# Denominators of a graph attention: some weight tiles summed on GpSimd, fewer by ones on TensorE, and the transfers' sum closed in the next block

## The chip, the cores and the metric

One core of a Trainium2 chip runs the whole program. The metric is the device time of one execution in microseconds, the median of three; the profile is one profiled execution of the same program. The engines are named as in the profile: PE is TensorE, DVE is VectorE, ACT is ScalarE, POOL is GpSimd, SP is the engine whose queue issues most of the loads.

## The reference

Two graph layers work on 4096 nodes with 512 features each and one adjacency matrix of 4096 x 4096 zeros and ones. Each has four heads of 128 features. The change concerns the second layer, a graph attention:

```python
feats = jnp.einsum('nf,hfo->hno', X, W)
e_s = jnp.einsum('hno,ho->hn', feats, a_self)
e_n = jnp.einsum('hno,ho->hn', feats, a_neigh)
logits = e_s[:, :, None] + e_n[:, None, :]
logits = jnp.where(logits > 0, logits, LRELU_ALPHA * logits)
logits = logits + NEG_INF * (1.0 - A)[None, :, :]
attn = jax.nn.softmax(logits, axis=-1)
out = jnp.einsum('hnm,hmo->hno', attn, feats)
```

X is the normalised output of the first layer. For every target node n the softmax needs, besides the weighted sum over its neighbours m, the sum of the weights themselves: the denominator.

## The kernel before

The program runs a first stage (normalisation, projections), an encoder attention, a feed-forward block, a decoder attention, a second block, and at the end the attention of the second layer ("gat"). All three attentions share one function, `attention` (L210).

Its work is cut into blocks: one head h and one half tb of the targets (TB = 2048 targets), eight blocks for each attention. Inside a block a loop goes over j, 32 tiles of 128 neighbours. For each j a weight tile e of 128 neighbours x 2048 targets in fp32 (1 MB) is made: ACT computes it from a row of target scores (L798), and DVE adds a column and multiplies with the mask (L799, `gat_weights`); the mask `a` is one byte an element and is loaded by SP's queue. Then TensorE multiplies the values' 128 x 128 tile with the four 512-wide parts of e and accumulates over j in four PSUM banks `po` (`products`, L351; fp32, so a product appears as two matmul instructions). In the first tiles of a block only three of the four banks are free, and the fourth catches up at j = EVICT = 2 (L348).

The denominators are the column sums of all 32 weight tiles, and there are three ways for a tile to get into them. `modes(n)` says which for block n; before the change all eight blocks of the last attention use `GAT` (L64):

- *moved* (11 tiles): GpSimd issues a transfer that adds the tile, element by element, onto a tile `sums2` (L363). In the first block it is added onto a DRAM tile `dacc`, which is loaded back into a weight tile at j = 30 (L319 to L321), because `sums2` shares the memory of the first block's row. Each transfer waits for the one before it, since both change the same tile.
- *by ones* (3 tiles: 9, 30, 31): TensorE multiplies with a 128 x 32 matrix of ones and accumulates into a PSUM bank `den` (`add_to_den`, L303): four 512-wide parts side by side in four groups of 32 columns, eight instructions a tile.
- all others (18 tiles): DVE adds them to `acc` (L369 the first two, L371 the rest), which is half of the big tile R[2].

At j = 31, `sums2` and `acc` go through the ones as well, so that `den` then holds the denominators (L378 to L382).

What is to be done after a block is put into `later`, a table by tile number of the next block: at j = EVICT ACT copies the four banks out (`out_gat`, L804); at j = INVERT = 4 ACT copies `den`, and GpSimd's queue writes it to DRAM and reads it back as a column (`denominators`, L244 to L251); at j = 10 DVE takes the reciprocals and GpSimd's queue writes them (L253 to L256); from j = 11 GpSimd's queue loads them spread over all partitions (rb, L261), and six tiles later DVE multiplies the block's results with them (L808), ACT applies the bias and the ReLU (L811), and GpSimd's queue adds them to the output (L817). In the last block there is no next one, and the end is done at once (L394 to L411).

The order of instructions on each engine is that of the program's text with some pins (`tc.issue_after`). The sum by ones goes behind the products of its tile, and the next products behind it. Weight tiles go round in a ring: EP + ebufs = 2 + 7 = 9 tiles in the last attention (`weight_tile`, L237). A tile is free again when its products, and its transfer or its add, are done.

Of the kernel before, what the change touches and what calls it, by code (L numbers as in the profile page):

```python
# [31 lines left out]
FP = mybir.dt.float32  # L32
U8 = mybir.dt.uint8
AF = mybir.ActivationFunctionType
ALU = mybir.AluOpType
# [4 lines left out]
N, F, H, D, P = 4096, 512, 4, 128, 128  # L40
IB = 512
NIB = N // IB
NJ = N // P
C = IB // P

TB = 2048
NTB = N // TB
SB = TB // IB
# [8 lines left out]
TINY = 1e-30  # L57
# [1 line left out]
G_MAX = 75.0  # L59


ENC_FIRST = (), (5, 6, 10, 11, 15, 16, 20, 21, 25, 26, 30, 31)
ENC = (0, 2, 5, 7, 10, 12, 15, 17, 20, 22, 25), (8, 9, 30, 31)
GAT = (0, 2, 5, 7, 10, 12, 15, 17, 20, 22, 25), (9, 30, 31)  # L64

KEEP = 5

# [2 lines left out]
EVICT = 2  # L70
INVERT = 4
# [9 lines left out]
def kernel(ctx, tc, x, xT, adjT, w0, w0T, v0, wencT, wdecT, vecs, w1, w1T, a1, outT):  # L81
    nc = tc.nc
    consts = ctx.enter_context(tc.tile_pool(name="consts", bufs=1))
    dram = ctx.enter_context(tc.tile_pool(name="dram", bufs=1, space=DRAM))
# [5 lines left out]
    R = [big.tile([P, N], FP, name=f"R{i}") for i in range(5)]  # L90
# [12 lines left out]
    def bank1():  # L103
        return psum1.tile([P, IB], FP, name="den")
# [3 lines left out]
    ones = consts.tile([P, P], FP, name="ones")  # L108
# [38 lines left out]
    ekeep = [[[dram.tile([P, TB], FP, name=f"ekeep{h}_{t}_{k}") for k in range(NJ // KEEP)] for t in range(NTB)]  # L147
             for h in range(H)]

    dacc = dram.tile([P, TB], FP, name="dacc")  # L150

    masks = [[dram.tile([MG * P, TB], U8, name=f"mask{t}_{g}") for g in range(NJ // MG)] for t in range(NTB)]

    def everywhere(d, row, lo, n):
# [55 lines left out]
    def attention(what, keep, pools, weights, values, row_of, out, finish, ebufs, modes=None, invert=None,  # L210
# [21 lines left out]
        spool, made, masks0 = pools, 0, list(masks0)  # L232
        if invert is not None:
            acc = spool.tile([P, TB], FP, name="acc") if sums is None else sums
            sums2 = spool.tile([P, TB], FP, name="acc2") if sums2 is None else sums2

        def weight_tile():  # L237
            nonlocal made
            made += 1
            if made % (EP + ebufs) < EP:  # L240
                return keep.tile([P, TB], FP, name="e", tag="ek", bufs=EP)
            return spool.tile([P, TB], FP, name="e", bufs=ebufs)
# [15 lines left out]
        def spread(h, tb, s):  # L258
# [2 lines left out]
            nc.gpsimd.dma_start(rb, everywhere(rinvs[h][tb], 0, s * IB, IB))  # L261
            return rb

        def at(j, f, *args):

            later.setdefault(j, []).append(lambda: f(*args))

        def ending(h, tb, po, den):

            outs = [out(spool, h, tb, s, po[s]) for s in range(SB)]  # L270
            if den is not None:
                def invert_later():
                    dcol = denominators(h, tb, den)
                    at(INVERT + 6, invert_them, h, tb, dcol)

                at(INVERT, invert_later)
            rbs = {}
            for s, o in enumerate(outs):

                j = INVERT + 7 + s % 2 + s // 2 * 7  # L280
                at(j, lambda s=s: rbs.update({s: spread(h, tb, s)}))
                for k, f in enumerate(finish):
                    at(j + 6 + k, lambda f=f, s=s, o=o: f(spool, h, tb, s, o, rbs[s], False))
# [8 lines left out]
        blocks = [(h, tb) for h in range(H) for tb in range(NTB)]  # L292
        for n, (h, tb) in enumerate(blocks):
            last = n == len(blocks) - 1
            moved, by_ones = modes(n) if modes is not None else ((), ())
            if invert is not None:
                den = bank1()
                begun = False

            def add_to_den(t, stop=False):  # L300
                nonlocal begun, last_ones
                for s in range(SB):
                    last_ones = nc.tensor.matmul(den[s * 32:(s + 1) * 32, :], ones[:, 0:32], t[:, s * IB:(s + 1) * IB],  # L303
                                                 start=not begun, stop=stop)
                begun = True

            po, ahead = [bank() for _ in range(SB - 1)], []
            adds, held, back, stores, next_row = [], [], None, [], None
            for j in range(NJ):

                with pinned(products_of):
                    for f in later.pop(j, []):
                        f()
                with tc.issue_after(a_load.ins) if j else nullcontext():
                    if (n, j) in extras:
                        extras[n, j](a_load)
                    if not last and j == NJ - 10:
                        next_row = next_row_of(*blocks[n + 1])
                if n == 0 and moved and j == NJ - 2:  # L319
                    back = weight_tile()  # L320
                    nc.gpsimd.dma_start(back, dacc)  # L321
                e = weight_tile()
                store = j % KEEP == KEEP - 1 and kept is not None
                if store and kept == "read":
                    a_load = nc.sync.dma_start(e, ekeep[h][tb][j // KEEP])
                else:
                    if masks0:
                        a, a_load = masks0.pop(0)
                    else:
                        a = mask_tile(keep)  # L330
                        a_load = load_mask(a, tb, j)
                    products_of = weights(e, rowb, a, j, h, SB if n + j == 0 else 1)
                    if store:
                        stores.append((j // KEEP, e))

                    if j % KEEP == KEEP - 3 and stores:
                        k, t = stores.pop()
                        nc.scalar.dma_start(ekeep[h][tb][k], t)

                def products():  # L340
                    nonlocal last_main, last_ones

                    with tc.issue_after(last_ones.ins) if last_ones is not None else nullcontext():

                        if j == EVICT:
                            po.append(bank())
                            for k, t in ahead:
                                nc.tensor.matmul(po[-1], block(values[h], k), t[:, (SB - 1) * IB:SB * IB],  # L348
                                                 start=(k == 0), stop=False)
                        for s, b in enumerate(po):  # L350
                            last_main = nc.tensor.matmul(b, block(values[h], j), e[:, s * IB:(s + 1) * IB],  # L351
                                                         start=(j == 0), stop=(j == NJ - 1))
                    last_ones = None


                early = last and j == NJ - 1 and invert is not None
                if not early:
                    products()
                if j < EVICT:
                    ahead.append((j, e))  # L360
                if invert is not None:
                    if j in moved:
                        nc.gpsimd.dma_start(sums2 if n else dacc, e, **({"accum_op": ALU.add} if j > moved[0] else {}))  # L363
                    elif j in by_ones:
                        held.append(e)
                    else:
                        adds.append(e)
                        if len(adds) == 2:
                            nc.vector.tensor_add(acc, *adds)  # L369
                        elif len(adds) > 2:  # L370
                            nc.vector.tensor_add(acc, acc, e)  # L371

                    if held and j + 1 not in by_ones:
                        with tc.issue_after(last_main.ins):
                            for t in held:
                                add_to_den(t)
                        held = []
                    if j == NJ - 1:  # L378
                        with tc.issue_after(last_ones.ins) if last_ones is not None else nullcontext():
                            if moved:  # L380
                                add_to_den(sums2 if n else back)
                            add_to_den(acc, True)  # L382
                if early:
                    products()
            for k, t in stores:
# [2 lines left out]
                else:  # L388
                    at(EVICT, nc.scalar.dma_start, ekeep[h][tb][k], t)
            if not last:  # L390
                at(EVICT, lambda *block_end: ending(*block_end), h, tb, po, den if invert is not None else None)
                rowb = next_row
                continue
            outs = [out(spool, h, tb, s, po[s]) for s in range(SB)]  # L394
# [31 lines left out]
    with tc.tile_pool(name="keep", bufs=1) as keep:  # L426

        with tc.tile_pool(name="f_small", bufs=1) as small, tc.tile_pool(name="f_work", bufs=2) as work:
# [5 lines left out]
            for ib in range(NIB):  # L434
# [7 lines left out]
                for c in range(0, C, 1 if ib == 0 else C):  # L442
                    n = 1 if ib == 0 else C
# [375 lines left out]
    with tc.tile_pool(name="gat", bufs=1) as spool:  # L819
        x1_last = []  # L820

        def load_last(load):
            x1_last.append(spool.tile([P, TB], FP, name="rowb", bufs=2))
            nc.sync.dma_start(x1_last[0], outT[(H - 1) * P:H * P, (NTB - 1) * TB:NTB * TB])

        attention("gat", spool, spool, gat_weights, v1, lambda h, tb: (rowsg, tb * H + h), out_gat,
                  (scaled_gat, add_to_output), 7, lambda n: GAT, (N * TINY, ALU.add), sums=R[2][:, 0:TB],
                  sums2=row0, row0=row0,
                  extras={(H * NTB - 1, NJ - 10): load_last})


# [40 lines left out]
```

## Time and profile before

| | |
|---|---|
| median of three runs | 3309.0 us (3308.68 to 3311.59) |
| profiled span | 3308.6 us, granted TensorE clock 0.989 |
| last attention | from about 2366 us to the end, 943 us |
| TensorE busy in it | 928 us |
| VectorE busy in it | 908 us |
| ScalarE busy in it | 571 us |
| GpSimd busy in it | 126 us, all of it issuing transfers |
| transfer that adds a weight tile | 1 MB, 8.2 us from issue to landing |

The profile has several views. The page gives busy time by engine, the span in 40 equal slices and the chain of work that ended last. Groups of instructions are listed by line and shape as "busy us, mean ns of one | idle us of the engine just before them, and what ended that idle time". The timeline lists instructions by start and duration, equal neighbours merged ("x8"). A busy TensorE is not TensorE at its peak, since ends of matmuls are modelled; its pace is best read from the starts of successive blocks. An instruction that stands still after it has begun, because something it needs is taken, counts as busy and shows only as a longer duration.

### The profile page before, as it was taken

Reading aid. Unit: us, or ns where it says so; the run is one execution under the profiler, and the core shown is the slowest. Engines: PE = TensorE matmul, PEld = TensorE weight load, DVE = VectorE, ACT = ScalarE, POOL = GpSimd, SP = SyncE. Lnnn points to the kernel's source line nnn. Section 1 sums busy time; section 2 is a strip of 40 time slices with the busy share of each in tenths; the row PEclk is TensorE's granted clock in tenths of the full one; section 3 lists DMA queues with packets and bytes.
Section 4 is the critical chain, followed back from the end, with each engine's and each line's share of the span. In section 5 each row is a group of like instructions: output and inputs, shape, how many; then the busy total and the mean of one; then the engine's idle time right before and its main releaser. Section 6 shows DMA issues by size and latency. Waiting matters only on the chain.

```text
span 3308.6 us, 25868 instructions
## 1 busy us (share of the span) xinstructions
PE 3226.6 (98%) x8847; PEld 1492.2 (45%) x8847; DVE 2677.1 (81%) x1912; ACT 2602.9 (79%) x1908; POOL 329.1 (10%) x478
## 2 busy tenths in 40 slices
PE   7989999999999999999999999999999999999999
PEld 6434434434443464444444444448644444444443
DVE  6989899999998675555655666586599989999997
ACT  7999999999997448999999999565656566566563
POOL 2000110110110000000000000024201111111111
PEclk9999999999999999999999999999999999999999
DMA  9994888988986013333443443232389779778876
GB/s 207 196 187 147 249 225 231 248 224 227 248 238 186 4 45 137 135 129 137 152 140 124 137 153 133 66 134 75 82 199 223 174 194 221 192 193 208 216 190 147
DMA packets 180164, 558.54 MB, mean 169 GB/s; under 512 B 20356, under 2 KB 23684, under 8 KB 144192
## 3 DMA queue, kind: packets, MB, share of 16 engines
q0 software_dynamic: 43088, 210.09, 32.9%
q1 hardware_dynamic: 126288, 293.66, 26.2%
q10 hardware_dynamic: 10656, 53.15, 4.0%
q8 instruction: 69, 1.13, 0.1%
q14 instruction: 63, 0.52, 0.0%
HBM read 378.15 MB, written 95.82 MB: 143 GB/s over the span
## 4 chain that ended last, share of the span: by engine, by line
PE 67%; DVE 16%; issue 9%; ACT 5%; DMA 3%; DVEq 0%; ACTq 0%; POOL 0%; POOLq 0%
PE ps L351 52%; PE ps L566 7%; DVE e L421 4%; DVE e L799 4%; DVE R L371 4%; PE ps L743 3%; ACT e L419 2%; PE den L303 2%; DVE acc L371 2%; ACT e L420 2%; DMA a<-mask 2%; PE ps L622 1%; PE ps L348 1%; PE ps L500 1%; DMA rb<-rinvs 1%
## 5 line engine op out<-in xcount | busy, mean ns | idle before, releaser
L351 PE MATMUL ps<-e,R 128*128 128x512 f32 x6048 | 2640.7, 597 | 51.8 <-DVE e L421 39.9
L351 PEld LDWEIGHTS ps<-e,R 128*128 128x128 f32 x6048 | 1147.4, 191 | 1536.4 <-issue 1417.3
L421 DVE TENSOR_TENSOR e<-e,a 128x2048 f32<-128x2048 f32 (+1 forms) x470 | 1052.3, 2260 | 403.6 <-ACT e L420 381.6
L419 ACT ACTIVATE e<-rowb,score 128x2048 f32<-128x2048 f32 (+1 forms) x470 | 912.6, 1968 | 91.3 <-PE ps L351 58.0
L420 ACT ACTIVATE e<-e 128x2048 f32<-128x2048 f32 (+1 forms) x470 | 871.0, 1880 | 17.5 <-DVE e L421 11.1
L798 ACT ACTIVATE e<-rowb,nq,jcol 128x2048 f32<-128x2048 f32 x224 | 457.9, 2086 | 225.2 <-DMA w<-e 130.1
L799 DVE SCALAR_TENSOR_TENSOR e<-e,jcol,a 128x2048 f32<-128x2048 f32 (+1 forms) x259 | 591.5, 2319 | 4.5 <-DMA a<-mask 2.7
L371 DVE TENSOR_TENSOR R<-R,e 128x2048 f32<-128x2048 f32 x128 | 292.5, 2285 | 0.0
L371 DVE TENSOR_TENSOR acc<-acc,e 128x2048 f32<-128x2048 f32 x126 | 287.9, 2285 | 1.8
L566 PE MATMUL ps<-R,w 128*128 128x512 f32 x512 | 220.3, 592 | 0.6 <-DVE w L534 0.6
L261 POOL DMA_DIRECT2D rb<-rinvs x88 | 58.7, 683 | 1095.6 <-DVE R L524 904.8
L566 PEld LDWEIGHTS ps<-R,w 128*128 128x128 f32 x512 | 97.2, 190 | 122.7 <-issue 118.2
L363 POOL DMA_DIRECT2D w<-e x77 | 64.6, 839 | 643.6 <-DMA w<-e 267.5
L743 PE MATMUL ps<-w1x,hT 128*128 128x260 f32 x512 | 119.6, 393 | 1.8 <-ACT hT L717 1.8
L586 ACT ACTIVATE ex<-ps,bias 128x512 f32<-128x512 f32 x64 | 44.0, 688 | 95.5 <-PE ps L566 78.4
L363 POOL DMA_DIRECT2D acc<-e x66 | 55.6, 842 | 607.7 <-DMA acc<-e 225.7
L743 PEld LDWEIGHTS ps<-w1x,hT 128*128 128x128 f32 x512 | 99.2, 195 | 22.0 <-ACT hT L717 3.4
L798 ACT ACTIVATE e<-w,nq,jcol 128x2048 f32<-128x2048 f32 (+1 forms) x35 | 65.6, 1938 | 30.1 <-DMA dacc<-e 28.6
L811 ACT ACTIVATE R<-R,vec 128x512 f32<-128x512 f32 x32 | 23.0, 719 | 72.4 <-DVE R L808 72.3
L588 DVE SCALAR_TENSOR_TENSOR ex<-ex,re 128x512 f32<-128x512 f32 x64 | 45.0, 703 | 35.7 <-ACT re L587 35.5
L748 ACT ACTIVATE R<-ps,rstd 128x128 f32<-128x128 f32 x128 | 38.0, 367 | 42.4 <-PE ps L743 42.4
L303 PE MATMUL den<-e,ones 128*32 128x512 f32 x584 | 70.9, 599 | 0.0
(158 smaller groups left out, 1265.1 us busy)
## 6 DMA issues: line engine op xcount, KB each, us to landing
a<-mask SPq DMA_DIRECT2D x720, 256.0 KB, 3.5
w<-e POOLq DMA_DIRECT2D x77, 1024.0 KB, 8.2
acc<-e POOLq DMA_DIRECT2D x66, 1024.0 KB, 8.6
ekeep<-e ACTq DMA_DIRECT2D x48, 1024.0 KB, 5.5
e<-ekeep SPq DMA_DIRECT2D x48, 1024.0 KB, 4.9
rb<-rinvs POOLq DMA_DIRECT2D x88, 256.0 KB, 5.7
mask<-in_adjT POOLq DMA_DIRECT2D x8, 2048.0 KB, 103.3
rowb<-rows SPq DMA_DIRECT2D x16, 1024.0 KB, 4.9
```

The source lines that it names most:

```text
L261: nc.gpsimd.dma_start(rb, everywhere(rinvs[h][tb], 0, s * IB, IB))
L303: last_ones = nc.tensor.matmul(den[s * 32:(s + 1) * 32, :], ones[:, 0:32], t[:, s * IB:(s + 1) * IB], start=not begun, stop=stop)
L351: last_main = nc.tensor.matmul(b, block(values[h], j), e[:, s * IB:(s + 1) * IB], start=(j == 0), stop=(j == NJ - 1))
L363: nc.gpsimd.dma_start(sums2 if n else dacc, e, **({"accum_op": ALU.add} if j > moved[0] else {}))
L371: nc.vector.tensor_add(acc, acc, e)
L419: nc.scalar.activation(e, rowb, AF.Tanh, bias=column(score[:, 1], j, h), scale=0.5)
L420: last_act = nc.scalar.activation(e, e, AF.Exp, scale=0.5)
L421: last_dve = nc.vector.tensor_mul(e, e, a)
L566: nc.tensor.matmul(z, w[:, fb, o * P:(o + 1) * P], nodes(src[fb], ib), start=(fb == 0), stop=(fb == C - 1))
L743: nc.tensor.matmul(b[:, 0:2 * DX], hT[:, fb, c * P:(c + 1) * P], w1x[:, fb, 2 * k:2 * k + 2, :].rearrange("p h x -> p (h x)"), start=(fb = ...
L798: last_act = nc.scalar.activation(e, rowb, AF.Relu, bias=column(nq, j, h), scale=column(jcol, j, h))
L799: last_dve = nc.vector.scalar_tensor_tensor(e, e, column(jcol2, j, h), a, ALU.add, ALU.mult)
```

## The change

The change gives the last attention a fourth way for a tile into the denominators: *pooled*. GpSimd adds such tiles to a new tile `acc3`, as DVE does to `acc`. Three tiles after the last pooled one, `acc3` itself is sent as one more adding transfer onto the transfers' sum. In exchange fewer tiles go by ones and fewer are added on DVE; the purpose is to take work from the two full engines and give it to the nearly empty one. `modes` now returns different lists for the first block, the six in the middle and the last block:

| block | moved | by ones | pooled | left to DVE |
|---|---|---|---|---|
| all, before | 11 | 3 | 0 | 18 |
| first, after | 10 | 2 | 5 | 15 |
| middle six, after | 11 | 0 | 6 | 15 |
| last, after | 8 | 2 | 5 | 17 |

In the middle blocks the last moved tile is tile 31. Its transfer can't have landed when the block ends, so only `acc` goes through the ones at j = 31, and the transfers' sum follows in the next block at j = INVERT + 1 = 5 (`ends_later`); copying and inverting the denominators moves back by two tiles. In the first block the transfers' sum now lies in the other half of R[2], so that the DRAM tile and its load disappear. The tile `acc3` costs a weight tile: `ebufs` goes from 7 to 6, the ring from nine to eight tiles. The lists of the encoder attention get an empty fourth entry; nothing else changes there.

```diff
+GAT_FIRST = (0, 2, 5, 7, 10, 12, 15, 17, 20, 22), (30, 31), (1, 6, 11, 16, 21)
+GAT = (6, 9, 11, 13, 16, 18, 21, 24, 27, 30, 31), (), (1, 4, 8, 14, 19, 23)
+GAT_LAST = (6, 8, 10, 13, 15, 18, 20, 22), (30, 31), (1, 4, 9, 14, 19)
-GAT = (0, 2, 5, 7, 10, 12, 15, 17, 20, 22, 25), (9, 30, 31)
...
-        def ending(h, tb, po, den):
+        def ending(h, tb, po, den, ends_later, into):
+            step = INVERT
+            if ends_later:
+                at(step + 1, add_to_den, den, into, False, True)
+                step += 2
...
+            ends_later = moved and moved[-1] > NJ - 3
+            into = sums2[0 if n else 1] if moved else None
...
-                if n == 0 and moved and j == NJ - 2:
-                    back = weight_tile()
-                    nc.gpsimd.dma_start(back, dacc)
...
                     if j in moved:
-                        nc.gpsimd.dma_start(sums2 if n else dacc, e, **({"accum_op": ALU.add} if j > moved[0] else {}))
+                        nc.gpsimd.dma_start(into, e, **({"accum_op": ALU.add} if j > moved[0] else {}))
                     elif j in by_ones:
                         held.append(e)
                     else:
-                        adds.append(e)
-                        if len(adds) == 2:
-                            nc.vector.tensor_add(acc, *adds)
-                        elif len(adds) > 2:
-                            nc.vector.tensor_add(acc, acc, e)
+                        some, total, engine = ((pool_adds, acc3, nc.gpsimd) if j in pooled else (adds, acc, nc.vector))
+                        some.append(e)
+                        if len(some) == 2:
+                            engine.tensor_add(total, *some)
+                        elif len(some) > 2:
+                            engine.tensor_add(total, total, e)
+                    if pooled and j == pooled[-1] + 3:
+                        nc.gpsimd.dma_start(into, acc3, accum_op=ALU.add)
...
-                            if moved:
-                                add_to_den(sums2 if n else back)
-                            add_to_den(acc, True)
+                            if moved and not ends_later:
+                                add_to_den(den, into, not begun)
+                                begun = True
+                            add_to_den(den, acc, not begun, not ends_later)
...
-                  (scaled_gat, add_to_output), 7, lambda n: GAT, (N * TINY, ALU.add), sums=R[2][:, 0:TB],
-                  sums2=row0, row0=row0,
+                  (scaled_gat, add_to_output), 6,
+                  lambda n: (GAT_FIRST, *[GAT] * (H * NTB - 2), GAT_LAST)[n], (N * TINY, ALU.add), sums=R[2][:, 0:TB],
+                  sums2=(row0, R[2][:, TB:N]), row0=row0,
```

More of the change, by code (lines that the diff above doesn't have):

```diff
@@ L59 @@
 G_MAX = 75.0
-ENC_FIRST = (), (5, 6, 10, 11, 15, 16, 20, 21, 25, 26, 30, 31)
-ENC = (0, 2, 5, 7, 10, 12, 15, 17, 20, 22, 25), (8, 9, 30, 31)
-GAT = (0, 2, 5, 7, 10, 12, 15, 17, 20, 22, 25), (9, 30, 31)
+ENC_FIRST = (), (5, 6, 10, 11, 15, 16, 20, 21, 25, 26, 30, 31), ()
+ENC = (0, 2, 5, 7, 10, 12, 15, 17, 20, 22, 25), (8, 9, 30, 31), ()
+GAT_FIRST = (0, 2, 5, 7, 10, 12, 15, 17, 20, 22), (30, 31), (1, 6, 11, 16, 21)
+GAT = (6, 9, 11, 13, 16, 18, 21, 24, 27, 30, 31), (), (1, 4, 8, 14, 19, 23)
+GAT_LAST = (6, 8, 10, 13, 15, 18, 20, 22), (30, 31), (1, 4, 9, 14, 19)
 KEEP = 5
@@ L148 @@
              for h in range(H)]
-    dacc = dram.tile([P, TB], FP, name="dacc")
     masks = [[dram.tile([MG * P, TB], U8, name=f"mask{t}_{g}") for g in range(NJ // MG)] for t in range(NTB)]
@@ L234, in attention @@
             acc = spool.tile([P, TB], FP, name="acc") if sums is None else sums
-            sums2 = spool.tile([P, TB], FP, name="acc2") if sums2 is None else sums2
+            sums2 = (spool.tile([P, TB], FP, name="acc2"), None) if sums2 is None else sums2
+            if any(modes(n)[2] for n in range(H * NTB)):
+                acc3 = spool.tile([P, TB], FP, name="acc3")
         def weight_tile():
@@ L262, in spread, with add_to_den @@
             return rb
+        def add_to_den(den, t, start=False, stop=False):
+            nonlocal last_ones
+            for s in range(SB):
+                last_ones = nc.tensor.matmul(den[s * 32:(s + 1) * 32, :], ones[:, 0:32], t[:, s * IB:(s + 1) * IB],
+                                             start=start, stop=stop)
         def at(j, f, *args):
             later.setdefault(j, []).append(lambda: f(*args))
-        def ending(h, tb, po, den):
+        def ending(h, tb, po, den, ends_later, into):
[3 more added lines that the diff above has]
+                step += 2
             outs = [out(spool, h, tb, s, po[s]) for s in range(SB)]
@@ L273, in invert_later @@
                     dcol = denominators(h, tb, den)
-                    at(INVERT + 6, invert_them, h, tb, dcol)
-                at(INVERT, invert_later)
+                    at(step + 6, invert_them, h, tb, dcol)
+                at(step, invert_later)
             rbs = {}
             for s, o in enumerate(outs):
-                j = INVERT + 7 + s % 2 + s // 2 * 7
+                j = step + 7 + s % 2 + s // 2 * 7
                 at(j, lambda s=s: rbs.update({s: spread(h, tb, s)}))
@@ L294, in attention @@
             last = n == len(blocks) - 1
[L295 to L305, printed above, removed]
+            moved, by_ones, pooled = modes(n) if modes is not None else ((), (), ())
+            den = bank1() if invert is not None else None
+            ends_later = moved and moved[-1] > NJ - 3
+            into = sums2[0 if n else 1] if moved else None
+            begun = False
             po, ahead = [bank() for _ in range(SB - 1)], []
-            adds, held, back, stores, next_row = [], [], None, [], None
+            adds, pool_adds, held, stores, next_row = [], [], [], [], None
             for j in range(NJ):
@@ L375, in attention @@
                             for t in held:
-                                add_to_den(t)
+                                add_to_den(den, t, not begun)
+                                begun = True
                         held = []
@@ L379, in attention @@
                         with tc.issue_after(last_ones.ins) if last_ones is not None else nullcontext():
-                            if moved:
-                                add_to_den(sums2 if n else back)
-                            add_to_den(acc, True)
+                            if moved and not ends_later:
+                                add_to_den(den, into, not begun)
+                                begun = True
+                            add_to_den(den, acc, not begun, not ends_later)
                 if early:
@@ L390, in attention @@
             if not last:
-                at(EVICT, lambda *block_end: ending(*block_end), h, tb, po, den if invert is not None else None)
+                at(EVICT, ending, h, tb, po, den, ends_later, into)
                 rowb = next_row
```

## The prediction

> **What bounds the kernel now.** First the page's busy shares and slices, to see which engine is full where.
>
> ```profile
> PE 3226.6 (98%) x8847; PEld 1492.2 (45%) x8847; DVE 2677.1 (81%) x1912; ACT 2602.9 (79%) x1908; POOL 329.1 (10%) x478
> ...
> DVE  6989899999998675555655666586599989999997
> ...
> POOL 2000110110110000000000000024201111111111
> ```
>
> A slice is 3308.6/40 = 82.7 us. TensorE (PE) is full nearly everywhere; in the last eleven or so slices, which are the attention that the change touches, VectorE (DVE) is full as well and GpSimd (POOL) nearly empty. So I read that stage, 2366 to 3309 us (943 us), by groups of instructions, first DVE, then TensorE (columns: busy us, mean ns of one | idle us before them and releaser).
>
> ```profile
> L799 DVE SCALAR_TENSOR_TENSOR e<-e,jcol,a 128x2048 f32<-128x2048 f32 x255 | 588.7, 2344 | 1.2 <-ACT e L798 1.2
> L371 DVE TENSOR_TENSOR R<-R,e 128x2048 f32<-128x2048 f32 x128 | 292.5, 2285 | 0.0
> L808 DVE TENSOR_TENSOR R<-R,rb 128x512 f32<-128x512 f32 x28 | 19.2, 687 | 14.3 <-DMA rb<-rinvs 14.3
> ```
>
> Between its first tiles and its last mask product DVE idles 14.3 us in all, and only for the spread reciprocals (rb). Instructions overlap a little: in the timeline a mask product (L799) is followed after 2.265 us and an add (L371) after 2.205. A block is then 32 x 2.265 + 17 x 2.205 + 4 x 0.61 (L808) + 0.2 = 112.6 us, and the starts of the blocks' first add, 2961.68, 3074.08 and 3186.48, are 112.4 apart. Next the chain of waits (start, us, step).
>
> ```profile
> 2775.62 2.34 DVE e L799
> 2806.62 4.59 DVE e L799 x3
> 2822.36 2.58 DMA a<-mask
> 2831.32 3.70 PE ps L351 x8
> 2835.02 3.57 PE den L303 x32
> 2838.59 5.35 PE ps L351 x12
> 2845.66 27.47 PE ps L351 x64
> 2874.12 75.73 PE ps L351 x176
> 2949.85 3.57 PE den L303 x32
> ```
>
> Up to 2831 us it runs through DVE, afterwards through TensorE, whose block is 2949.85 - 2835.02 = 114.83 us. The two engines are within 2% of each other: relieving TensorE alone gains little before DVE is met, and any time added on DVE above some 2.4 us a block shows in full.
>
> Last, does GpSimd disturb DVE? The only GpSimd adds of any size here are L671 and L673 (128x512, earlier in the run). The timeline of both engines:
>
> ```profile
> 2176.27 0.68 DVE L588 SCALAR_TENSOR_TENSOR ex<-ex,re 128x512 f32<-128x512 f32 x1
> 2176.42 1.65 POOL L671 TENSOR_TENSOR S<-R,x 128x512 f32<-128x512 f32 x1 [0.63 <-DVE x L669]
> 2176.98 1.65 DVE L591 TENSOR_TENSOR x<-R,ex 128x512 f32<-128x512 f32 x1
> 2178.66 0.69 DVE L594 BATCH_NORM_STATS2 stats<-x 128x6 f32<-128x512 f32 x1
> 2179.27 1.28 DVE L669 TENSOR_TENSOR x<-x,xt 128x512 f32<-128x512 f32 x2
> 2180.03 3.32 POOL L671 TENSOR_TENSOR S<-R,x 128x512 f32<-128x512 f32 x2 [1.95 <-DVE x L669]
> 2180.46 1.76 DVE L588 SCALAR_TENSOR_TENSOR ex<-ex,re 128x512 f32<-128x512 f32 x1
> 2182.26 1.64 DVE L591 TENSOR_TENSOR x<-R,ex 128x512 f32<-128x512 f32 x1
> ```
>
> Undisturbed, L588 and L591 take 0.69 and a GpSimd add 1.26 us. Here the GpSimd add waits for the DVE instruction under way, and the next DVE instruction, 1.65 to 1.76 instead of 0.69, ends some 0.55 us after the GpSimd add: they take turns. That holds for both DVE forms, tensor_tensor and scalar_tensor_tensor, which are the two that fill the last stage.
>
> **What the Trainium skill says.** "SBUF — State Buffer", section "SBUF: two separate sides": DVE and GpSimd share a pair of ports that is "an **exclusive lock**, not a bandwidth split"; a DVE operation with two SBUF inputs contends for it against a GpSimd operation that reads SBUF, the first gets it for its whole instruction and the other stands still. The lines above agree. "GPSIMD Engine Reference", section "3.1 Elementwise — side-by-side cycle accounting": a 2048-element fp32 add takes 4497 ns there and 2293 ns on DVE; the trace agrees for DVE (2285), and no 2048-element GpSimd add is in it.
>
> **The change part by part.** All of it lies in the last attention's eight blocks.
>
> *TensorE.* Tiles summed by ones, with the transfers' sum and acc, are 5 a block now; they become 4, six times 2, and 4: 20 tiles fewer. One is 8 matmul instructions, and 32 take 3.57 us, so 0.89 a tile: 20 x 0.89 = 17.8 us off TensorE, 2.7 a middle block (114.8 to 112.1).
>
> *DVE adds.* In all blocks now 32 - 11 moved - 3 by ones = 18 tiles, 17 adds. Afterwards first block 32 - 10 - 2 - 5 = 15 tiles, 14 adds; middle 32 - 11 - 6 = 15, 14 adds; last 32 - 8 - 2 - 5 = 17, 16 adds. That is 3 + 6 x 3 + 1 = 22 adds fewer, 22 x 2.205 = 48.5 us off DVE.
>
> *GpSimd adds.* Pooled tiles less one: 4 + 6 x 5 + 4 = 38 adds of 128x2048. Own time: the trace has 0.453 us for 128 elements (L754, median 0.455) and 1.26 for 512, so 2.10 ns an element, and 1.26 + 1536 x 0.0021 = 4.49 us, as the skill has it. What DVE loses by one: six disturbed DVE instructions (1.65, 1.64, 1.64, 1.64, 1.76, 1.75) are 1.0 us over their 0.69, less than the 1.26 because the start-up overlaps; at 2048 elements 1.0 + 3.23 = 4.23 us. Bounds: 2.2 (if half of an add ran free beside DVE) and 4.5. I take 4.23, because DVE in this stage has nothing but operations with two SBUF inputs, back to back. 38 x 4.23 = 160.7 us onto DVE.
>
> *DVE's sum.* 160.7 - 48.5 = +112 us; by block, first +10.3, middle 6 x 14.6, last +14.7. A middle block becomes 127 us of DVE against 112 of TensorE: DVE carries the path alone. Off that: the lag that TensorE now has behind DVE at the end. The last mask product is done at 3283.6, its matmuls start at 3294.4; with TensorE waiting they start after the four den tiles (3.6) and some backlog, about 6 us earlier. And part of the 14.3 us of rb waits may vanish, because a longer block gives them more time, or stay; I take off 4. So 3309 + 112 - 6 - 4 = 3411.
>
> *Transfers' sum ending in the next block.* The added wait: TensorE's matmuls on the sum, placed at the next block's tile 5 (the 20 products of tiles 0 to 4 ahead of them, some 18 us), wait for tile 31's transfer, itself queued behind tile 30's. Behind them in TensorE's queue are tile 5's products; ACT's copy of den and the next block's first transfer (tile 6, onto the same tile) wait for them. TensorE has 15 us of slack a block by then, and the copy is used some 15 tiles later: nothing. On GpSimd's queue 11 transfers and the one of acc3, at about 9 us each (8.2 to landing, 0.84 to issue) are 109 of 127 us; the 4.5 us adds are queued between a transfer and the next, which waits for the landing anyhow, so they cost no time there; a GpSimd add itself waits for its tile's mask product, which DVE has done by then. But rinvs and rb are queued behind them, and DVE's L808 waits for rb: that is rival 2.
>
> *Eight weight tiles instead of nine, the first block's sum in SBUF instead of DRAM.* At 4 us a tile, eight tiles are 32 us of turnover, against a tile held for about 9 to 20 us by its transfer; ACT has over a third of the stage free (571 of 943 us busy). The removed load of the DRAM sum was not in the chain. Nothing for both.
>
> **The rivals.** (1) *No lock where it matters*: GpSimd adds run free beside DVE. DVE's block falls to 106, TensorE bounds throughout: 3309 - 17.8 = 3291. For it: the mask is one byte an element, which no instruction of the timeline above had. Against: both fp32 forms were stopped. (1b) *Only the adds are stopped, not the mask product with its byte mask*: a GpSimd add then hides under the next mask product, and costs 2.0 us where an add follows, in 3 of 5 cases: 38 x 0.6 x 2.0 = 46, against 48.5 saved: DVE about as now, less TensorE's lag: 3300. (2) *The lock, and GpSimd's queue late as well*: its longest rb wait now is 8.7 us; if each of the seven block ends waits so long, 61 instead of 14, 3411 + 47 = 3458. For it: GpSimd's queue already waits 267 us for landings. Against: the block is 13% longer.
>
> **How the numbers follow.** The lock at 4.2 us an add, 3411: 0.72. Lock and late queue, 3458: 0.13. Rival 1b, 3300: 0.06; rival 1, 3291: 0.09. With 3.4 us an add the first case gives 3411 - 38 x 0.83 = 3380, with 4.5 it gives 3421; the range is 3380 to 3460, which leaves rivals 1 and 1b and the tails out. Faster 0.13, same 0.02 (part of 1b), slower 0.85.
>
> **What would show it.** GpSimd adds of 4.5 to 6.8 us (with the wait for the DVE instruction under way); mask products or adds of about 6.5 us, one for each GpSimd add; the chain through DVE in all eight blocks; TensorE idle by some 15 us a middle block, waiting for the mask product; blocks' first adds 127 us apart. Mask products that stay at 2.34 beside a GpSimd add would overturn it, and waits for rb of over 30 us would show rival 2.

## The result and the profile after

The kernel after takes 3412.7 us (3411.9 to 3413.7), the one before 3308.8 in the runs beside it: a ratio of 1.0314, 95% interval 1.0298 to 1.0329, so 104 us slower. The page of the kernel after, first its busy shares and slices:

```profile
PE 3242.8 (95%) x8687; PEld 1489.7 (44%) x8687; DVE 2790.7 (82%) x1890; ACT 2597.6 (76%) x1908; POOL 562.5 (16%) x519
...
DVE  6989999999987765665566554965999999999998
...
POOL 2000111111010000000000000233323433433432
```

In the last stage GpSimd is now busy for two to four tenths of a slice, mostly one before, and DVE stays full although 22 adds were taken from it. The stage now lasts from 2366 to 3411 us. Its groups of instructions on DVE and GpSimd (lines have moved: L809 is the mask product that was L799, L377 the adds on both engines, L818 was L808; columns as before: busy us, mean ns of one | idle us before them and releaser). The first line is the mask product of the kernel before, in both its shapes; the others are of the kernel after:

```profile
L799 DVE SCALAR_TENSOR_TENSOR e<-e,jcol,a 128x2048 f32<-128x2048 f32 (+1 forms) x259 | 591.5, 2319 | 4.5 <-DMA a<-mask 2.7
...
L809 DVE SCALAR_TENSOR_TENSOR e<-e,jcol,a 128x2048 f32<-128x2048 f32 (+1 forms) x259 | 723.5, 2830 | 12.9 <-ACT e L808 10.7 <-DMA a<-mask 2.2
...
L377 DVE TENSOR_TENSOR R<-R,e 128x2048 f32<-128x2048 f32 x106 | 262.9, 2480 | 1.0
L377 POOL TENSOR_TENSOR acc<-acc,e 128x2048 f32<-128x2048 f32 x30 | 182.3, 6078 | 135.5 <-DVE e L809 135.5
...
L375 POOL TENSOR_TENSOR acc<-e 128x2048 f32<-128x2048 f32 x8 | 52.6, 6569 | 38.9 <-DVE e L809 38.9
...
L818 DVE TENSOR_TENSOR R<-R,rb 128x512 f32<-128x512 f32 x28 | 23.4, 834 | 1.2 <-DMA rb<-rinvs 1.2
```

All three DVE groups have grown longer on average: the mask product from 2319 ns (both shapes) to 2830, the add from 2285 to 2480, the multiplication with rb from 687 to 834. Times their counts that is 132.3 + 20.7 + 4.1 = 157.1 us, or 4.13 us for each of the 38 GpSimd adds. The idle time for rb, 14.3 us before, is 1.2. Where the growth sits is seen in the timeline of the two engines, GpSimd first:

```profile
2908.26 6.43 POOL L377 TENSOR_TENSOR acc<-acc,e 128x2048 f32<-128x2048 f32 x1 [13.55 <-DVE e L809]
...
2932.78 6.58 POOL L377 TENSOR_TENSOR acc<-acc,e 128x2048 f32<-128x2048 f32 x1 [3.51 <-DVE e L809]
```

```profile
2908.03 2.28 DVE L377 TENSOR_TENSOR R<-R,e 128x2048 f32<-128x2048 f32 x1
2910.23 11.13 DVE L809 SCALAR_TENSOR_TENSOR e<-e,jcol,a 128x2048 f32<-128x2048 f32 x3
2921.29 2.28 DVE L377 TENSOR_TENSOR R<-R,e 128x2048 f32<-128x2048 f32 x1
...
2932.72 2.25 DVE L809 SCALAR_TENSOR_TENSOR e<-e,jcol,a 128x2048 f32<-128x2048 f32 x1
2935.01 6.50 DVE L377 TENSOR_TENSOR R<-R,e 128x2048 f32<-128x2048 f32 x1
```

The GpSimd add at 2932.78 begins while a mask product (2932.72) is under way, waits for it, and ends at 2939.36. The DVE add queued at 2935.01 ends at 2941.51, so it took 6.50 instead of 2.28 us: 4.22 too long. At 2910.23 the victim is a mask product with its byte mask: three take 11.13 instead of 6.87, 4.26 too long. Both forms are stopped. Over the whole stage 37 DVE instructions are lengthened so, 31 mask products of 5.9 to 7.4 us, 5 adds of 6.5 and a multiplication with rb of 5.0: one for each of the 38 GpSimd adds but one.

The chain of waits, which the profile follows back to 2615 us and so through the last six blocks, runs mainly through DVE to the last product. At the start of each of them it also passes through the landing of a transfer, and in the last block through GpSimd's queue (parts of it; start, us, step):

```profile
2888.62 8.05 DMA w<-e
...
3199.58 4.61 DVE e L809 x2
...
3209.37 2.26 DVE e L809
...
3219.00 6.66 DVE e L809
...
3227.89 11.12 DVE e L809 x3
3239.54 2.28 DVE R L377
```

The sum of DVE over the stage settles the account. Busy times by engine in the stage, before and then after:

```profile
2366.00:3308.60 942.60, 927.57 (x2377) 398.54 (x2377) 907.88 (x451) 570.80 (x335) 126.43 (x166) 0.99 0.81 197
```

```profile
2366.00:3411.30 1045.30, 944.24 (x2216) 397.05 (x2216) 1020.68 (x425) 564.75 (x333) 359.42 (x207) 0.97 0.75 180
```

The third time is DVE's: 907.9 us busy before, 1020.7 after, so 112.8 more; idle 34.7 before and 24.6 after, so 10.1 less. Together 102.7 us, which is the difference of the two spans. (The lengthened instructions less 22 adds of 2.205 give 108.6 of the 112.8. The rest is mostly that neighbours on DVE overlap less than before, by 29.1 us in all instead of 36.6.) The last three numbers are the granted TensorE clock, the share of the transfer engines and GB/s.

### The profile page after: what moved, and what is told of

Its sections match the earlier page's. It is cut to its first block, busy times and chain, and to the rows that moved or that the text cites. A ratio compares the mean times of both kernels' runs of the same rounds, so it can differ in the third digit from the quotient of the medians.

```text
span 3411.3 us, 25605 instructions
## 1 busy us (share of the span) xinstructions
PE 3242.8 (95%) x8687; PEld 1489.7 (44%) x8687; DVE 2790.7 (82%) x1890; ACT 2597.6 (76%) x1908; POOL 562.5 (16%) x519
## 5 line engine op out<-in xcount | busy, mean ns | idle before, releaser
L356 PE MATMUL ps<-e,R 128*128 128x512 f32 x6048 | 2665.1, 600 | 113.4 <-DVE e L809 67.4
L809 DVE SCALAR_TENSOR_TENSOR e<-e,jcol,a 128x2048 f32<-128x2048 f32 (+1 forms) x259 | 723.5, 2830 | 12.9 <-ACT e L808 10.7
L808 ACT ACTIVATE e<-rowb,nq,jcol 128x2048 f32<-128x2048 f32 x224 | 455.2, 2085 | 247.3 <-DMA w<-e 212.0
L377 DVE TENSOR_TENSOR acc<-acc,e 128x2048 f32<-128x2048 f32 x126 | 287.8, 2284 | 1.8
L377 DVE TENSOR_TENSOR R<-R,e 128x2048 f32<-128x2048 f32 x106 | 262.9, 2480 | 1.0
L377 POOL TENSOR_TENSOR acc<-acc,e 128x2048 f32<-128x2048 f32 x30 | 182.3, 6078 | 135.5 <-DVE e L809 135.5
L808 ACT ACTIVATE e<-w,nq,jcol 128x2048 f32<-128x2048 f32 (+1 forms) x35 | 65.9, 1939 | 34.9 <-DMA R<-e 25.5
L353 PE MATMUL ps<-e,R 128*128 128x512 f32 x96 | 56.2, 710 | 24.2 <-ACT R L814 24.1
```

What stands on the lines that cost most here:

```text
L377: engine.tensor_add(total, total, e)
L808: last_act = nc.scalar.activation(e, rowb, AF.Relu, bias=column(nq, j, h), scale=column(jcol, j, h))
L809: last_dve = nc.vector.scalar_tensor_tensor(e, e, column(jcol2, j, h), a, ALU.add, ALU.mult)
```

## Experiments: is it the adds on GpSimd?

The theory is the lock: each GpSimd add takes about 4.2 us from DVE, which can do nothing else in that time. The rivals were the smaller ring of weight tiles, and GpSimd's queue with its longer chain of transfers and the late sum.

**The pooled tiles on DVE.** The engine that adds is another. With no tile pooled, `acc3` and its transfer, the twelfth of a block, fall away too; eight tiles, the late sum and the other lists stay:

```diff
-GAT = (6, 9, 11, 13, 16, 18, 21, 24, 27, 30, 31), (), (1, 4, 8, 14, 19, 23)
+GAT = (6, 9, 11, 13, 16, 18, 21, 24, 27, 30, 31), (), ()
```

(and the same in GAT_FIRST and GAT_LAST).

> The kernel after, with the pooled tiles added on DVE instead of GpSimd (first 19, middle 20, last 21 adds); nine-to-eight ring, late sum and new lists stay. Lock theory (each GpSimd add takes 4.2 us from DVE): 24 DVE adds more than before, 24 x 2.205 = +53 us, less some 6 to 10 us of lag and waits: 3346 to 3356 us, 60 us faster than the kernel after although DVE does 46 more adds. Rival, ring or queue (eight tiles, late sum and long transfer chain hold the engines): no better than the kernel after, 3410 or more.

Measured: 3340.4 us (3339.0 to 3342.5), 1.0094 of the kernel before, interval 1.0079 to 1.0109. DVE does 46 adds more than in the kernel after and the program is 72 us faster. This run alone can't tell the adds from the twelfth transfer; the doubled adds below can. The starts of the blocks' first add are 2967.14, 3086.18 and 3205.78: 119.0 and 119.6 us a block, where 32 x 2.265 + 20 x 2.205 + 2.7 gives 119.3. The total is 6 us under the expected range; the wait for rb is gone here (none is recorded, 14.3 us before) and DVE's last wait for the denominators fell from 11.0 to 2.9 us, which the expectation had only partly taken off.

**Eight tiles alone.**

```diff
-                  (scaled_gat, add_to_output), 7, lambda n: GAT, (N * TINY, ALU.add), sums=R[2][:, 0:TB],
+                  (scaled_gat, add_to_output), 6, lambda n: GAT, (N * TINY, ALU.add), sums=R[2][:, 0:TB],
```

> The kernel before with one change: eight weight tiles instead of nine. Lock theory: 3309 to 3314 us. Ring theory: at least half of the 104 us that the change cost, 3360 or more.

Measured: 3310.9 us, 1.0004, interval 0.9996 to 1.0013. The smaller ring by itself costs the kernel before nothing that can be measured.

**The change without adds on GpSimd.**

```diff
-                        if len(some) == 2:
+                        if j in pooled:
+                            pass
+                        elif len(some) == 2:
...
-                    if pooled and j == pooled[-1] + 3:
-                        nc.gpsimd.dma_start(into, acc3, accum_op=ALU.add)
```

> The kernel after without the GpSimd adds and without the transfer of their sum; the pooled tiles are left out of the denominators. All else of the change stays: eight tiles, late sum, fewer tiles by ones, fewer DVE adds. Lock theory: TensorE bounds with 17.8 us less, 3291 to 3297 us. Ring or late sum theory: over 3350.

Measured: 3285.9 us, 0.9929, interval 0.9914 to 0.9944. That is 24 us under the kernel before where 17.8 were counted; the other 6 were not followed up. Two lines of its chain of waits, which is TensorE's, give the block:

```profile
3065.34 0.99 PE den L270 x8
...
3177.59 1.00 PE den L270 x8
```

112.25 us, against 114.83 before; the prediction had 112.1. So eight tiles, late sum and new lists, with eleven transfers a block, do no harm once the adds are gone, and the relief of TensorE is what was counted. What the adds and the transfer of their sum cost together is 3412.7 - 3285.9 = 126.8 us.

**Each add twice.** Right behind each GpSimd add the same add again:

```diff
                         elif len(some) > 2:
                             engine.tensor_add(total, total, e)
+                        if j in pooled and len(some) > 1:
+                            engine.tensor_add(total, total, e)
```

> The kernel after with each of the 38 GpSimd adds done twice in a row (denominators count these tiles twice). Lock theory with the 4.1 to 4.2 us an add that the trace after shows: 3413 + 38 x 4.15 = 3570 us, 3550 to 3590, with DVE instructions of some 6.5 us twice as often. If the slowdown came from the ring or the chain of transfers and the adds merely lay beside it: under 3450.

Measured: 3572.0 us (3570.5 and 3573.4). 38 more adds cost 159.2 us, 4.19 us each. That is the price of the disputed operation by itself.

## Experiments: what does the lock ask for?

**Fills for adds.** GpSimd writes as large a tile, twice, but reads nothing. A wait on the tile's mask product keeps it in its place:

```diff
-                        if len(some) == 2:
+                        if j in pooled and len(some) > 1:
+                            for k in range(FILLS):
+                                fill = nc.gpsimd.memset(total, 0.0)
...
+                        elif len(some) == 2:
```

> The kernel after with each GpSimd add replaced by two GpSimd fills of the same 128x2048 tile, which write and read nothing and wait for the same mask product; the pooled tiles are left out of the denominators. GpSimd stays busy for some 3 to 5 us each. Lock theory as the skill words it (only a GpSimd instruction that reads SBUF stops DVE): DVE's block is 106 us, TensorE bounds, 3291 to 3300 us. Lock by any GpSimd instruction: 38 fills pairs of some 3.5 us or more, 3370 or more. Queue theory (a busy GpSimd delays its transfers): about 3400.

Measured: 3346.8 us, 1.0108, interval 1.0092 to 1.0125: in none of the three ranges. The groups of its DVE and GpSimd instructions:

```profile
L817 DVE SCALAR_TENSOR_TENSOR e<-e,jcol,a 128x2048 f32<-128x2048 f32 (+1 forms) x259 | 591.3, 2319 | 78.7 <-ACT e L816 76.5 <-DMA a<-mask 2.2
...
L385 DVE TENSOR_TENSOR R<-R,e 128x2048 f32<-128x2048 f32 x106 | 242.4, 2286 | 1.0
L377 POOL MEMSET acc<- 128x2048 f32 x76 | 149.5, 1967 | 141.7 <-DVE e L817 140.2
```

About the lock they are plain: with GpSimd busy for 150 us, mask product and add stay at 2319 and 2286 ns, within 1 ns of the kernel before. A GpSimd instruction that only writes takes nothing from DVE, as the Trainium skill has it ("SBUF — State Buffer", "SBUF: two separate sides": only against a GpSimd operation that reads SBUF). But DVE idles for 76.5 us, waiting for weight tiles from ACT. So there is a second cost, which the lock mostly hides in the kernel after; it is taken up below.

**Copies for adds.** One SBUF input instead of two, and no transfer of the sum:

```diff
-                        if len(some) == 2:
+                        if j in pooled and len(some) > 1:
+                            engine.tensor_copy(total, e)
+                        elif len(some) == 2:
...
-                    if pooled and j == pooled[-1] + 3:
-                        nc.gpsimd.dma_start(into, acc3, accum_op=ALU.add)
```

> GpSimd copies the pooled tile (one SBUF input) instead of adding it (two), and the twelfth transfer is left out too; the pooled tiles are left out of the denominators. [...] Lock theory (any GpSimd read stops a DVE instruction with two SBUF inputs for its duration): DVE instructions of some 4 us, 106 + 5 x 1.6 = 114 us of DVE a block against 112 of TensorE: 3296 to 3310 us. If only two-input GpSimd instructions stop DVE: no long DVE instruction, 3286 to 3290 us.

Measured: 3316.4 us, 1.0021, interval 1.0013 to 1.0030. The timeline of this kernel's GpSimd, and then of its DVE:

```profile
2878.59 3.96 POOL L375 COPY acc<-e 128x2048 f32<-128x2048 f32 x1 [3.48 <-DVE e L809]
```

```profile
2878.54 2.25 DVE L809 SCALAR_TENSOR_TENSOR e<-e,jcol,a 128x2048 f32<-128x2048 f32 x1
2880.83 3.86 DVE L379 TENSOR_TENSOR R<-R,e 128x2048 f32<-128x2048 f32 x1
```

The copy begins while a mask product is under way, which ends at 2880.79, and ends itself at 2882.55: it ran for 1.76 us. The DVE add behind it takes 3.86 instead of 2.28, 1.58 too long. So reading one operand is enough to stop DVE, for nearly as long as the copy runs. (The same reading of the add at 2932.78 above gives 4.39 us of running and 4.22 of DVE's time.) By the group means, 259 x (2473 - 2319) + 106 x (2386 - 2285) ns = 50.6 us, 1.33 for each of the 38 copies; 32 DVE instructions are lengthened, to between 3.2 and 4.6 us. The total lies 6 us above the expected range and says little about the lock: its six middle blocks are 115.9 us apart on average, and so are those of the fills without the transfer of the sum (next section), where DVE is not stopped. The lengthened instructions are the evidence here.

## Experiments: the second cost

**Fills without the twelfth transfer.** As with the fills, less the two lines that send the sum:

```diff
-                    if pooled and j == pooled[-1] + 3:
-                        nc.gpsimd.dma_start(into, acc3, accum_op=ALU.add)
```

> The fills of the run before, without the twelfth transfer that carries the filled tile onto the sum (11 transfers a middle block; pooled tiles are left out of the denominators). Chain theory (twelve transfers that wait for one another, at some 9.6 us each, are 116 us, longer than the 112 us that a block then has): 3286 to 3293 us, as without fills. Busy theory (4 us of fills in front of a transfer delay it): 3330 or more.

**The twelfth transfer without fills.**

```diff
+                acc3 = spool.tile([P, TB], FP, name="acc3")
+                nc.gpsimd.memset(acc3, 0.0)
...
-                        if len(some) == 2:
+                        if j in pooled:
+                            pass
+                        elif len(some) == 2:
```

> The counterpart: the twelfth transfer, of a tile of zeros, without fills or adds on GpSimd (pooled tiles left out of the denominators). Chain theory: 3335 to 3347 us. Busy theory: 3286 to 3293 us.

Measured: 3306.0 us (3303.2 to 3310.6) and 3324.0 us (3320.2 to 3328.6). Neither expectation held alone. Against the 3285.9 without either, fills cost 20.1 and the transfer 38.1 us, together 58.2; the run with both cost 60.9. The two add up.

What the fills do is seen in GpSimd's queue (the run without the transfer):

```profile
2851.23 3.67 POOL L377 MEMSET acc<- 128x2048 f32 x2 [15.10 <-DVE e L815]
2854.85 0.55 POOL L369 DMA_DIRECT2D w<-e  x1
```

The fills of tile 4 wait for its mask product, and the block's first transfer, of tile 6, stands behind them. The transfers' sum went through the ones at 2846.09, so that this transfer could have started some 7 us earlier. That this is where all of the 20 us come from was not tested.

**The twelfth transfer with nine tiles.** Its source is a resident tile, so that no weight tile is lost:

```diff
-                        nc.gpsimd.dma_start(into, acc3, accum_op=ALU.add)
+                        nc.gpsimd.dma_start(into, values[h][:, 0:TB], accum_op=ALU.add)
...
-                  (scaled_gat, add_to_output), 6,
+                  (scaled_gat, add_to_output), 7,
```

> The twelfth transfer without fills again, but its source is a resident tile of the values, so that no tile is spent on it and the ring has nine weight tiles (pooled tiles left out of the denominators, into which values come instead). If the 38 us that the twelfth transfer cost with eight tiles are the chain's own length (twelve times 9.6 us or more): 3318 to 3328 us again. If the chain is short enough and eight tiles were too few to ride out its lateness: 3286 to 3298 us.

Measured: 3317.6 us (3309.8 to 3322.8), 1.0023, interval 1.0013 to 1.0032. Of the 38 us the ninth tile gives back about 6 (the intervals of the two runs just touch); most of the cost is there without it. The issues of the transfers in this kernel, one block to the first of the next (start, us of the issue):

```profile
2854.53 0.55 POOL L367 DMA_DIRECT2D w<-e  x1 [15.04 <-PE den L270]
2860.17 0.94 POOL L367 DMA_DIRECT2D w<-e  x1
...
2928.31 0.85 POOL L381 DMA_DIRECT2D w<-R  x1 [6.73 <-DMA w<-e]
...
2954.11 0.85 POOL L367 DMA_DIRECT2D w<-e  x1 [7.13 <-issue]
2972.92 0.55 POOL L367 DMA_DIRECT2D w<-e  x1 [17.96 <-DVE R L378]
```

The twelve issues of a block take 2954.11 - 2854.53 = 99.6 us, 9.05 us from one to the next, and all but one of them come within 1.1 us of the landing before. To the next block's first it is 18.8 us more, together 118.4 us, where TensorE needs 112. What happens in the 18.8 us is seen in ACT and TensorE:

```profile
2963.66 12.03 ACT L810 ACTIVATE e<-rowb,nq,jcol 128x2048 f32<-128x2048 f32 x6 [5.59 <-DMA w<-e]
```

```profile
2971.53 1.06 PE L270 MATMUL den<-w,ones 128*32 128x512 f32 x8
```

The last transfer lands at 2963.58, 9.47 us after its issue, and frees its weight tile; ACT, which had waited for that, goes on with the next block's tiles at 2963.66. TensorE gets to tile 5 and to the ones behind it at 2971.53, and only then may tile 6's transfer overwrite the sum, at 2972.92: in all six such places of this trace it is issued 1.4 us after the ones begin. So the late sum closes a loop, and the ring of weight tiles is part of it. The ones themselves never waited for the landing, which came 6 to 9 us before them each time.

**Twelve tiles moved, nothing on GpSimd.** A whole kernel, to see whether a longer list of transfers pays:

```diff
+GAT_FIRST = (0, 2, 5, 7, 10, 12, 15, 17, 20, 22, 25), (9, 30, 31), ()
+GAT = (6, 8, 11, 13, 15, 18, 20, 23, 25, 27, 29, 31), (3, 9), ()
+GAT_LAST = (6, 8, 10, 13, 15, 17, 20, 22, 25), (2, 4, 11, 30, 31), ()
...
-                  (scaled_gat, add_to_output), 6,
+                  (scaled_gat, add_to_output), 7,
```

> A whole kernel without GpSimd adds: nine tiles, late sum, the middle blocks with 12 tiles moved, 2 by ones, 18 on DVE (before: 11, 3, 18). By the sums TensorE has 0.85 us less a middle block and DVE the same: 3303 to 3306 us. If twelve transfers in a chain are longer than a block of 114 us: 3315 to 3335 us, slower than before.

Measured: 3335.4 us, 1.0081, interval 1.0064 to 1.0098, slower than before, in line with the loop of the run ahead: the first transfers of three successive blocks are issued at 2740.50, 2857.91 and 2975.05, 117 us apart. It is also slower than that run. Its lists differ in more than the length: it sums tile 3 by ones, and TensorE waits 11.9 us there, in six waits, for ACT's copy of the denominators of the block before. How much that costs was not followed up. No complete kernel among these runs beats the one before.

## Why the prediction was right

Forecast 3411, measured 3412.7. Its terms, one by one:

- **What bounds the stage.** TensorE at 114.8 and DVE at 112.6 us a block, so that time added on DVE shows. It does: DVE's busy time grew by 112.8 us and the span by 102.7.
- **TensorE's relief**, 2.7 us a middle block: 2.6 in the run without adds (112.25), where TensorE bounds. In the kernel after TensorE idles 95 us of the stage, so the relief shows nothing there.
- **DVE's adds**, 2.205 us each: the run with the pooled tiles on DVE has blocks of 119.0 to 119.6 us, the sum gave 119.3.
- **The GpSimd add**, 4.23 us of DVE's time, extrapolated from adds a quarter as wide: 4.13 by the lengthened instructions, 4.19 by doubling the adds, 4.24 by DVE's busy time ((112.8 + 48.5)/38).
- **DVE's sum**, +112: the windows show +112.8. A middle block was to become 127 us of DVE. The six of them take 128.9 on average, from the first add at 2504.78 to that at 3278.37; the first of them, with 134.8, is the longest.
- **Taken off**, 6 for TensorE's lag and 4 for rb: 10.1 in all, but here the sum fits by luck. DVE's last wait for the denominators shrank from 11.0 to 2.9 (8.1), rb from 14.3 to 1.2 (13.1, three times the 4), and against that waits for new weight tiles, put at nothing, rose from 1.8 to 10.7.
- **TensorE idle by some 15 us a middle block**, as a sign: the groups show 71 us before the main products and 24 before the catching-up ones, 12 a block. The granted clock in the stage was 0.97 (0.99 before), and a main product took 604 ns on average (595 before).
- **Rival 2**, GpSimd's queue late: 1.2 us of rb waits and 2.0 for the denominators' column, so no.
- **Late sum, twelfth transfer and eight tiles at no cost.** Nearly true of this kernel: the waits for weight tiles rose by 9 us, and twelve transfers fit into its blocks. Two steps of the reasoning were wrong: DVE hasn't done the mask product "by then". GpSimd's adds wait 174 us for mask products (135.5 + 38.9 in the groups above), and the first transfer of a middle block behind another comes some 18 us after the last landing of that one, right behind the add of tile 4. Nor did TensorE's ones wait for tile 31's transfer, which landed 6 to 9 us before them. And the fit hung on the lock. In a block of 112 us the twelve don't fit (the runs above: up to 61 us with the fills). So rival 1's figure, 3291 without a lock, was wrong in its size: with adds that stop nobody I would now put the change near the 3347 us of the fills (an estimate from that run, not a measurement of it), slower than before as well. What that figure lacked is in "at about 9 us each ... 109 of 127 us": it counts twelve transfers to the last landing and leaves out some 10 us more, from that landing to the first transfer of the next block (118.4 against 109).

## What to carry to other kernels

A quiet engine is only help if it doesn't use what the full one uses: a 2048-element add moved to GpSimd spared DVE 2.2 us and cost it 4.2, and two engines within 2% of each other leave no room for that. Look in the trace for a place where both already run, however small: a quarter-sized add and six lengthened instructions gave this one's price to within 3%. And a chain of transfers onto one tile is a loop that includes its reader and the tiles that it holds: count from the first transfer to the first of the next round, not the transfers alone.

## What was not expected

GpSimd fills of 1.97 us, 76 of them, leave DVE's durations the same to a nanosecond, while a one-input copy stops DVE like an add. And the granted TensorE clock, 1.00 over the middle blocks before, is 0.97 over those after, in which TensorE pauses some 12 us a block.
